# A two-layer attention block on one core: 64 by 64 array tiles in the first attention, and softmax denominators inverted across partitions

## Chip, cores and metric

The kernel runs on one core of one Trainium2 chip. The metric is the device time of one launch in microseconds; the kernel before took 3954.51 us (median of three runs, 3954.51 to 3957.84).

## What is computed

The input is 16 images of 256 channels and 1024 positions in float32. Two layers follow each other for every image:

```python
# layer 0: 4 heads of 64
qkv = (xs @ w_proj + b_proj).reshape(B, S, 4, 3 * 64)
attn = softmax(einsum('bihd,bjhd->bijh', q, k) * 64 ** -0.5, axis=2)
res = einsum('bijh,bjhd->bihd', attn, v).reshape(B, S, 256) @ w_out + b_out + xs
# layer 1: 8 heads of 32
x = x + attention(group_norm(x, gn1_w, gn1_b), qkv_w, proj_w, proj_b, phys_bias)
h = gelu(einsum('oc,bchw->bohw', mlp_w1, group_norm(x, gn2_w, gn2_b)) + mlp_b1)
x = x + einsum('oc,bchw->bohw', mlp_w2, h) + mlp_b2
```

A softmax divides each weighted sum by the sum of its exponentials. That sum, one number for each head and each query position, is called the denominator below.

## The kernel before

Channels lie on the 128 partitions in two chunks (`CC = 2`), positions along the free dimension in blocks of 128 keys (`SB = 8`) and of 512 queries (`NT = 2`). `first_pass` does all the work; `general_pass` runs only if a range test on the denominators fails, which it does not do in the profiled execution. The test needs, for every denominator, a sum of the values and a sum of `exp(-den / 1e-20)`, which the ScalarE instructions at L326 and L329 deliver through `accum_out`; the second of them is called the range exponential below.

**Attention.** One function serves both layers. For a unit (a query block, a channel chunk, a key block) `scores` multiplies keys by queries into a PSUM tile of 128 by 1024 (L267), cut into pieces of 64 output partitions. ScalarE takes the exponential into an SBUF tile `e` (L279). `weigh` multiplies `e` by the values, over all 128 keys at once, into an accumulator bank (L288), and VectorE adds `e` into a running sum `es` (L305). After eight key blocks an item is done: ScalarE copies the accumulator to `res` (L310), and `normalise` follows two ticks later. It multiplies `es` by a matrix of ones, so that every partition of a head gets that head's denominator (L317), copies it out (L326), takes the range exponential (L329), the reciprocal on VectorE over 128 by 512 (L332) and multiplies `res` by it (L333). The second layer uses the same steps with four heads to a chunk and two score tiles per unit.

**Array tiles.** A TensorE instruction names the rows and columns of the array that it uses; the profile shows them as rows*columns. Float32 matmuls show as two instructions each. In the first attention the scores use 64*64 (four side by side), the weighted sums, the denominators and whatever goes through `product` use 128*64 (two side by side). In the second attention it is 32*64 and 128*32. Between the attentions `product` uses 128*128. `product` (L234) cuts its output into pieces of `cols[0]` columns.

**Order.** The image loop runs, for image b: first attention of b; the MLP's first half of image b-1 (`hidden`, L536, 8 pieces); queries, keys and values of layer 1; second attention of b, with pieces filled in between its units (the MLP's second half of b-1, L234 and L561, and the layer-0 projections of b+1). A small class `Later` holds work back by a number of ticks. A tick is one step of the attention generator (three units in the first attention, one in the second) or one piece. So the output projections, `out_proj`, run a few ticks behind their items: `o` for layer 0 and `j` for layer 1. The projection of the first query block of `o` falls near the end of the first attention, that of the second among the `hidden` pieces; the second of `j` falls into the next image's first attention. The tile framework then fixes each engine's instruction order at build time[...].

**Buffers.** PSUM holds three 128 by 1024 tiles, taken in rotation by `wide` (scores, projections, MLP), and two banks, taken by `bank` (accumulators, denominators, group-norm averages). SBUF has eight `e` tiles, four `es` and one `d` tile. SyncE issues the loads of x and the stores of the output and nothing else.

Of the kernel before, what the change touches and what calls it, by code (L numbers as in the profile page):

```python
# [14 lines left out]
P = 128  # L15
# [173 lines left out]
def first_pass(ctx, tc, x, out, k):  # L189
# [7 lines left out]
    work = ctx.enter_context(tc.tile_pool(name="work", bufs=2))  # L197
    small = ctx.enter_context(tc.tile_pool(name="small", bufs=2))
    ps_s = ctx.enter_context(
        tc.tile_pool(name="ps_s", bufs=3, space=bass.MemoryType.PSUM)  # L200
    )
    ps_a = ctx.enter_context(
        tc.tile_pool(name="ps_a", bufs=2, space=bass.MemoryType.PSUM)
    )

    def wide(name):
        return ps_s.tile([P, 2, TB], F32, tag="s", name=name)

    def bank(name):
        return ps_a.tile([P, TB], F32, tag="acc", name=name)  # L210

    blocks = 2 * B * NT * CC
    dsum = act.tile([P, blocks], F32, name="dsum")
    lsum = act.tile([P, blocks], F32, name="lsum")
    block = iter(range(blocks))
# [23 lines left out]

    def attention(layer, b, D, qT, kT, v_of, ones_of, scale, project):
        key = f"{layer}_{b}"
        G = P // D

        items = [(t, c) for t in range(NT) for c in range(CC)]
        if G > 2:
            items.sort(key=lambda tc: tc[1])
        units = [(i, kb) for i in range(len(items)) for kb in range(SB)]
        per = 6 // G
        steps = [units[n : n + per] for n in range(0, len(units), per)]
        res = []
        if G == 2:
            res.append(act.tile([P, CC, S], F32, tag="res", name=f"res_{key}"))
        accs, held, sums = {}, {}, {}  # L260

        def scores(i, kb):
            t, c = items[i]
            tiles = [wide(f"s_{key}_{i}_{kb}_{n}") for n in range(G // 2)]
            for g in range(G):
                for h in range(0, P, HALF):
                    nc.tensor.matmul(  # L267
                        tiles[g // 2][h : h + HALF, g % 2, :],
                        kT[g * D : (g + 1) * D, c, kb * P + h : kb * P + h + HALF],
                        qT[g * D : (g + 1) * D, c, t * TB : (t + 1) * TB],  # L270
                        start=True,
                        stop=True,
                    )
            es = []
            for n, s in enumerate(tiles):
                e = work.tile(
                    [P, 2, TB], F32, tag="e", name=f"e_{key}_{i}_{kb}_{n}", bufs=8
                )
                nc.scalar.activation(e, s, AF.Exp, scale=scale)  # L279
                es.append(e)  # L280
            return i, kb, es

        def weigh(i, kb, es):
            t, c = items[i]
            if kb == 0:
                accs[i] = bank(f"acc_{key}_{i}")
            for g in range(G):
                nc.tensor.matmul(  # L288
                    accs[i][g * D : (g + 1) * D, :],
                    v_of(c * G + g, kb),  # L290
                    es[g // 2][:, g % 2, :],
                    start=(kb == 0),
                    stop=(kb == SB - 1),
                )
            if kb == 0:
                held[i] = es
                return
            if kb == 1:
                sums[i] = [
                    work.tile([P, 2, TB], F32, tag="es", name=f"es_{key}_{i}_{n}", bufs=4)  # L300
                    for n in range(G // 2)
                ]
            for n, e in enumerate(es):
                d = sums[i][n]
                nc.vector.tensor_add(d, held[i][n] if kb == 1 else d, e)  # L305
            if kb == SB - 1:
                if not res:
                    res.append(act.tile([P, CC, S], F32, tag="res", name=f"res_{key}"))
                r = res[0][:, c, t * TB : (t + 1) * TB]
                nc.scalar.copy(r, accs.pop(i))  # L310
                later.after(2, lambda: normalise(i, r))

        def normalise(i, r):
            t, c = items[i]
            den = bank(f"den_{key}_{i}")
            for g in range(G):
                nc.tensor.matmul(  # L317
                    den[g * D : (g + 1) * D, :],
                    ones_of(c * G + g),
                    sums[i][g // 2][:, g % 2, :],  # L320
                    start=True,
                    stop=True,
                )
            at = next(block)
            d = work.tile([P, TB], F32, tag="d", name=f"d_{key}_{i}", bufs=1)
            nc.scalar.activation(  # L326
                d, den, AF.Identity, accum_out=dsum[:, at : at + 1]
            )
            nc.scalar.activation(  # L329
                den, den, AF.Exp, scale=-1.0 / DEN_MIN, accum_out=lsum[:, at : at + 1]  # L330
            )
            nc.vector.reciprocal(d, d)  # L332
            nc.vector.tensor_mul(r, r, d)  # L333
            if c == CC - 1:
                later.after(3, lambda: project(t, res[0]))

        cols[0] = D
        pending = []
        for step in steps:
            now = [scores(*u) for u in step]  # L340
            for p in pending:
                weigh(*p)
            pending = now
            yield
        for p in pending:
            weigh(*p)
        yield
        cols[0] = P

# [21 lines left out]
    def group_norm(key, src, stats, gw, gb, tag, out_tile, wait):  # L371
        st = {}

        def means():
            mv = small.tile([P, CC, 2], F32, tag="mv", name=f"mv_{key}")
            for cc in range(CC):
                nc.vector.bn_aggr(mv[:, cc, :], stats[:, cc].rearrange("p t k -> p (t k)"))
            mean_c = small.tile([P, CC], F32, tag="mean_c", name=f"mean_c_{key}")
            nc.vector.tensor_copy(mean_c, mv[:, :, 0])
            st.update(mv=mv, mean_c=mean_c)  # L380
            later.after(wait, variances)

        def variances():
            ps = bank(f"gm_{key}")
            product(ps[:, :CC], k["gavg"], st["mean_c"], start=True, stop=True)
            mean = small.tile([P, CC], F32, tag="mean", name=f"mean_{key}")
            nc.vector.tensor_copy(mean, ps[:, :CC])

            dv = small.tile([P, CC], F32, tag="dv", name=f"dv_{key}")
            nc.vector.tensor_sub(dv, st["mean_c"], mean)  # L390
            nc.vector.tensor_mul(dv, dv, dv)
            tv = small.tile([P, CC], F32, tag="tv", name=f"tv_{key}")
            nc.vector.tensor_add(tv, dv, st["mv"][:, :, 1])
            st.update(mean=mean, tv=tv)
            later.after(1, apply)

        def apply():
            ps = bank(f"gv_{key}")
            product(ps[:, :CC], k["gavg"], st["tv"], start=True, stop=True)
            rstd = small.tile([P, CC], F32, tag="rstd", name=f"rstd_{key}")  # L400
            nc.vector.tensor_scalar(rstd, ps[:, :CC], EPS, None, ALU.add)
            nc.gpsimd.tensor_tensor(rstd, rstd, k["mhalf"], ALU.pow)
            a = small.tile([P, CC], F32, tag="ga", name=f"ga_{key}")
            nc.vector.tensor_mul(a, rstd, gw)
            ma = small.tile([P, CC], F32, tag="gma", name=f"gma_{key}")
            nc.vector.tensor_mul(ma, st["mean"], a)
            c = small.tile([P, CC], F32, tag="gc", name=f"gc_{key}")
            nc.vector.tensor_sub(c, gb, ma)
            y = act.tile([P, CC, S], F32, tag=tag, name=f"gn_{key}")
            out_tile.append(y)  # L410
            for t in range(NT):
                sl = slice(t * TB, (t + 1) * TB)
                for cc in range(CC):
                    nc.vector.tensor_scalar(  # L414
                        y[:, cc, sl], src[:, cc, sl],
                        a[:, cc : cc + 1], c[:, cc : cc + 1], ALU.mult, ALU.add,
                    )
# [72 lines left out]
    def attention_0(b, qkv_tiles, xb, norm):  # L490
# [3 lines left out]
        def project(t, res):  # L494
# [5 lines left out]
            if t == NT - 1:  # L500
                norm(stats)

        return attention(
            "a", b, D0, q, kk, lambda h, kb: v[:, kb, h], lambda h: k["ones"],
            float(D0) ** -0.5, project,
        )

    def attention_1(b, qkv_tiles, xb, norm):
        q, kk, v = qkv_tiles
# [2 lines left out]
        def project(t, res):  # L512
            out_proj(
                f"j{b}", k["wpj"], CC,
                lambda kc: res[:, kc, t * TB : (t + 1) * TB],
                k["pjb"], xb, t, stats,
            )
            if t == NT - 1:
                norm(stats)

        return attention(
            "b", b, D1, q, kk, lambda h, kb: v[:, kb, h], lambda h: k["eones"][:, h],
            float(D1) ** -0.5, project,
        )

# [70 lines left out]


    def fold_bias():  # L600
        ps = bank("bvo")
        for co in range(CC):
            for kc in range(CC):
                nc.tensor.matmul(
# [11 lines left out]
    for b in range(B):  # L616
# [26 lines left out]
        for m, piece in enumerate(rest):  # L643
# [3 lines left out]
            attention_1(  # L647
                b, tiles1, xs[b],
                lambda st, b=b, hn=hn: group_norm(
                    f"h{b}", xs[b], st, k["g2w"], k["g2b"], "gn", hn, 2  # L650
                ),
            ),
            fill,
# [305 lines left out]
```

## Time and profile before

| | us |
|---|---|
| median of three runs | 3954.51 |
| the profiled execution | 3953.01 |
| its span | 3950.6 |
| PE busy in the span | 3923.9 |
| VectorE busy | 2461.4 |
| ScalarE busy | 2147.3 |
| one image, in the middle of the run (from one image's MLP start on PE, 1030.27, to the next's, 1274.58) | 244.31 |
| first attention of one image, about (PE, 1206.6 to 1274.6) | 68.0 |

The profiled execution spends 2.4 us outside its span. The page gives the engines' busy time, then the span in slices, the DMA queues, the chain of work that ended last, and groups of like instructions by line, engine and tile, with count, summed busy time, and mean duration in ns. The timeline lists an engine's instructions in order of time, with neighbours of one group merged: start, length, engine, line, operation, tiles, shape and count. Matmuls are pipelined, so the length of a merged group runs a little into the next one; differences between the starts of groups are exact.

### The profile page before, as it was taken

What the parts mean: (1) busy time and instruction counts of PE and PEld (TensorE: products, weight loads), DVE (VectorE), ACT (ScalarE), POOL (GpSimd) and SP (SyncE); (2) the same over time, 40 slices, a digit from 0 to 9 for tenths busy, and PEclk for the clock granted to TensorE, in tenths of its full rate; (3) what the DMA queues carried; (4) which work ended last, traced back from release to release, by engine and by line L of the source; (5) the groups of instructions that cost most, each with busy time, mean ns of one, the idle gap of its engine ahead of it and who ended that gap; (6) DMA issues with size and microseconds to landing.
All of it is one profiled execution on the core that took longest, in us unless ns stands there. A gap on an engine that the chain in (4) does not pass through costs nothing.

```text
span 3950.6 us, 77671 instructions
## 1 busy us (share of the span) xinstructions
PE 3923.9 (99%) x34685; PEld 1407.5 (36%) x34685; DVE 2461.4 (62%) x2539; ACT 2147.3 (54%) x2815; POOL 35.3 (1%) x58
## 2 busy tenths in 40 slices
PE   9999999999999999999999999999999999999998
PEld 3324333343333423334233342333424333343335
DVE  4684756847567475674756747567474665747672
ACT  4654645546455464554645546465564655646461
POOL 1000000000000000000000000000000000000000
PEclk9999999999999999999999999999999999999999
DMA  2000000000000000000000000000000000000000
GB/s 75 1 1 7 17 1 23 1 9 15 1 23 1 9 15 1 23 1 12 12 1 23 1 23 1 1 23 1 23 1 4 20 1 23 1 4 10 1 4 20
DMA packets 18501, 42.80 MB, mean 11 GB/s; under 512 B 3728, under 2 KB 5264, under 8 KB 18160
## 3 DMA queue, kind: packets, MB, share of 16 engines
q1 hardware_dynamic: 13824, 33.56, 2.4%
q8 instruction: 273, 4.47, 0.5%
q10 hardware_dynamic: 3712, 3.80, 0.3%
q0 software_dynamic: 624, 0.41, 0.1%
q14 instruction: 68, 0.56, 0.0%
HBM read 20.99 MB, written 16.78 MB: 10 GB/s over the span
## 4 chain that ended last, share of the span: by engine, by line
PE 98%; issue 1%; DVE 1%; DMA 0%; ACT 0%; POOL 0%; POOLq 0%; DVEq 0%
PE s_b L267 14%; PE acc_b L288 12%; PE s_a L267 12%; PE acc_a L288 12%; PE m L536 12%; PE m L234 11%; PE qk_b L234 6%; PE qk_a L234 5%; PE o L234 3%; PE v_a L234 3%; PE v_b L234 3%; PE j L234 3%; PE den_b L317 1%; PE den_a L317 1%; DVE es_b L305 0%
## 5 line engine op out<-in xcount | busy, mean ns | idle before, releaser
L279 ACT ACTIVATE e_b<-s_b 128x1024 f32<-128x1024 f32 x1024 | 994.2, 1025 | 615.7 <-PE s_b L267 608.7
L305 DVE TENSOR_TENSOR es_b<-es_b,e_b 128x1024 f32<-128x1024 f32 x768 | 895.0, 1221 | 296.6 <-ACT e_b L279 296.6
L267 PE MATMUL s_b<-q,k 32*64 32x512 f32 x8192 | 598.3, 613 | 5.0 <-DVE x L364 3.2
L279 ACT ACTIVATE e_a<-s_a 128x1024 f32<-128x1024 f32 x512 | 487.3, 1026 | 180.1 <-PE s_a L267 180.1
L288 PE MATMUL acc_b<-e_b,v 128*32 128x512 f32 x4096 | 546.0, 604 | 0.0
L305 DVE TENSOR_TENSOR es_a<-es_a,e_a 128x1024 f32<-128x1024 f32 x384 | 466.4, 1215 | 32.2 <-ACT e_a L279 5.5
L267 PE MATMUL s_a<-q,k 64*64 64x512 f32 x4096 | 479.8, 598 | 0.0
L288 PE MATMUL acc_a<-e_a,v 128*64 128x512 f32 x2048 | 477.4, 600 | 0.0
L536 PE MATMUL m<-gn_h,w 128*128 128x512 f32 x1024 | 474.8, 605 | 2.0 <-DVE gn_h L414 2.0
L234 PE MATMUL m<-g,w 128*32 128x256 f32 (+1 forms) x7616 | 464.7, 379 | 0.0
L234 PEld LDWEIGHTS m<-g,w 128*32 128x32 f32 (+1 forms) x7616 | 276.1, 112 | 219.1 <-issue 57.8
L544 ACT ACTIVATE g<-m,m1b 128x512 f32<-128x512 f32 x256 | 170.3, 686 | 317.8 <-PE m L536 317.4
L305 DVE TENSOR_TENSOR es_b<-e_b,e_b 128x1024 f32<-128x1024 f32 x128 | 151.1, 1222 | 234.1 <-ACT e_b L279 234.1
L536 PEld LDWEIGHTS m<-gn_h,w 128*128 128x128 f32 x1024 | 186.1, 190 | 256.4 <-issue 190.7
L267 PEld LDWEIGHTS s_b<-q,k 32*64 32x64 f32 x8192 | 144.8, 129 | 361.9 <-issue 178.8
L332 DVE RECIPROCAL d_a<-d_a 128x512 f32<-128x512 f32 x64 | 214.5, 3352 | 64.4 <-ACT d_a L326 64.4
L234 PE MATMUL qk_a<-x,wp 128*32 128x512 f32 (+1 forms) x1856 | 245.2, 594 | 8.8 <-DMA wp<-in_L_conv_w_proj_dram 6.7
L288 PEld LDWEIGHTS acc_a<-e_a,v 128*64 128x64 f32 x2048 | 132.7, 136 | 331.1 <-issue 331.1
L267 PEld LDWEIGHTS s_a<-q,k 64*64 64x64 f32 x4096 | 139.1, 132 | 304.1 <-issue 264.1
L234 PE MATMUL qk_b<-gn_g,wq 128*32 128x512 f32 (+1 forms) x1280 | 236.9, 593 | 0.0
L288 PEld LDWEIGHTS acc_b<-e_b,v 128*32 128x32 f32 x4096 | 82.2, 108 | 406.7 <-issue 402.5
L458 DVE TENSOR_TENSOR v<-v_b,eones 128x512 f32<-128x512 f32 x64 | 44.3, 692 | 276.2 <-PE v_b L234 276.2
(107 smaller groups left out, 2408.8 us busy)
## 6 DMA issues: line engine op xcount, KB each, us to landing
x<-in_x_dram SPq DMA_DIRECT2D x32, 512.0 KB, 4.5
out_dram<-x SPq DMA_DIRECT2D x64, 256.0 KB, 2.0
w<-in_L_conv_mlp_w_dram ACTq DMA_DIRECT2D x2, 1024.0 KB, 14.9
wq<-in_L_conv_qkv_w_dram ACTq DMA_DIRECT2D x1, 768.0 KB, 11.8
wp<-in_L_conv_w_proj_dram ACTq DMA_DIRECT2D x3, 128.0 KB, 9.7
wp<-in_L_conv_w_proj_dram POOLq DMA_DIRECT2D x3, 128.0 KB, 6.9
wo<-in_L_conv_w_out_dram ACTq DMA_DIRECT2D x1, 256.0 KB, 9.3
wpj<-in_L_conv_proj_w_dram ACTq DMA_DIRECT2D x1, 256.0 KB, 13.5
```

Of the source, the lines that this page charges most:

```text
L234: nc.tensor.matmul(o[sl], w[:, sl], r, **flags)
L267: nc.tensor.matmul(tiles[g // 2][h : h + HALF, g % 2, :], kT[g * D : (g + 1) * D, c, kb * P + h : kb * P + h + HALF], qT[g * D : (g + 1) * ...
L279: nc.scalar.activation(e, s, AF.Exp, scale=scale)
L288: nc.tensor.matmul(accs[i][g * D : (g + 1) * D, :], v_of(c * G + g, kb), es[g // 2][:, g % 2, :], start=(kb == 0), stop=(kb == SB - 1),)
L305: nc.vector.tensor_add(d, held[i][n] if kb == 1 else d, e)
L317: nc.tensor.matmul(den[g * D : (g + 1) * D, :], ones_of(c * G + g), sums[i][g // 2][:, g % 2, :], start=True, stop=True,)
L332: nc.vector.reciprocal(d, d)
L458: nc.vector.tensor_mul(d, ps, v_scale.unsqueeze(1).to_broadcast([P, 2, C // D, D]))
L536: nc.tensor.matmul(ps[:, n, :], k["w1"][:, cc, hc * P : (hc + 1) * P], hn[0][:, cc, t * TB : (t + 1) * TB], start=(cc == 0), stop=(cc == C ...
L544: nc.scalar.activation(g, ps[:, n, :], AF.Gelu, bias=k["m1b"][:, hc : hc + 1])
```

## The change

- **The first attention has a function of its own, `attention_a`.** The weighted sums are cut into two halves of 64 keys, each with 64 rows by 64 columns of the array, and the halves go to two PSUM banks. For every even item (counted from 0) the two banks come from `bank`; for every odd item they are the two halves of the third wide tile, which `kept` takes out of the rotation meanwhile. ScalarE copies the first half to `res` and VectorE adds the second. A tick is now one unit; the weighted sums run two units behind the scores.
- **Its denominators** are taken once per query block instead of once per item, with 32 columns and 256 queries to a matmul. `product` uses 32 columns in this stage instead of 64, and the group-norm averages in it use 64 rows by 64 columns.
- **The reciprocal in both attentions** goes through a new helper, `denominators`. ScalarE copies the denominators to `d`. SyncE then issues DMAs that lay one row per head (or half head) over partitions, so that VectorE inverts 128 by 16 instead of 128 by 512; DMAs that gather the results into rows `rr` on partitions 0 to 3; and DMAs that read each such row 64 times (first attention) or 32 times (second) to fill `full`, by which VectorE multiplies `res`.
- **The range exponential** works on `d` in place, after the DMAs that read it.
- **Ticks.** The second query block of `j` is projected in the middle of the next image's first attention, right before a denominator step; the first of `o` in the same attention, some units later; the second of `o` stays among the `hidden` pieces.
- `wide` rotates over three tags by hand; `es` has three buffers instead of four; `res` of layer 1 is two tiles, and the second group norm's output takes the buffer of `q1`.

```diff
+    def denominators(key, d, n, rows, out_to, waits, then, copy):
+        w = d.shape[1] * len(rows) // P
+        spread = work.tile([P, 2 * TB // D0], F32, tag="spread", name=f"sp_{key}", bufs=2)
+        spread = spread[:, :w]
+        rr = work.tile([4, TB], F32, tag="rr", name=f"rr_{key}", bufs=1)
+        full = work.tile([P, n, TB], F32, tag="full", name=f"rd_{key}", bufs=1)
+        at = next(block)
+        copy(at)
+        for p, lo, num, _ in rows:
+            nc.sync.dma_start(
+                spread[lo : lo + num], d[p : p + 1].rearrange("o (a b) -> o a b", b=w)
+            )
+
+        def invert():
+            nc.vector.reciprocal(spread, spread)
+            for *_, parts in rows:
+                for row, c0, lo, num in parts:
+                    nc.sync.dma_start(
+                        rr[row : row + 1, c0 : c0 + num * w].rearrange(
+                            "o (a b) -> o a b", b=w
+                        ),
+                        spread[lo : lo + num],
+                    )
+            for row, lo, num, c in out_to:
+                nc.sync.dma_start(
+                    full[lo : lo + num, c],
+                    rr[row : row + 1].unsqueeze(1).to_broadcast([1, num, TB]),
+                )
+            later.after(waits[1], lambda: then(full))
+
+        def low():
+            nc.scalar.activation(
+                d, d, AF.Exp, scale=-1.0 / DEN_MIN, accum_out=lsum[:, at : at + 1]
+            )
+
+        later.after(waits[0], invert)
+        later.after(waits[2], low)
...
+    def attention_a(b, qT, kT, v, project):
...
+            if kb == 0:
+                if i % 2:
+                    kept.add(2)
+                    acc = wide(f"acc_{key}_{i}", 2)
+                    accs[i] = [acc[:, h, :] for h in range(2)]
+                else:
+                    accs[i] = [bank(f"acc_{key}_{i}_{h}") for h in range(2)]
+            for h in range(2):
+                for g in range(2):
+                    nc.tensor.matmul(
+                        accs[i][h][g * D : (g + 1) * D, :],
+                        v[h * HALF : (h + 1) * HALF, kb, c * 2 + g],
+                        e[h * HALF : (h + 1) * HALF, g, :],
+                        start=(kb == 0),
+                        stop=(kb == SB - 1),
+                    )
...
+                nc.scalar.copy(r, one)
+                nc.vector.tensor_add(r, r, two)
+                kept.discard(2)
+                if c == CC - 1:
+                    later.after(1, lambda: normalise(t))
...
+                        nc.tensor.matmul(
+                            den[j : j + 32, c * half : (c + 1) * half],
+                            k["ones"][:, :32],
+                            sums[t * CC + c][:, g, h * half : (h + 1) * half],
...
+                (2, 3, 5) if t < NT - 1 else (1, 1, 26),
...
+        def scale(t, full):
+            r = res[:, :, t * TB : (t + 1) * TB]
+            nc.vector.tensor_mul(r, r, full)
+            later.after(1 if t < NT - 1 else 3, lambda: project(t, res))
...
+        cols[0] = 32
...
+    def attention_b(b, qT, kT, v, project):
...
-            nc.scalar.activation(
-                d, den, AF.Identity, accum_out=dsum[:, at : at + 1]
-            )
-            nc.scalar.activation(
-                den, den, AF.Exp, scale=-1.0 / DEN_MIN, accum_out=lsum[:, at : at + 1]
-            )
-            nc.vector.reciprocal(d, d)
-            nc.vector.tensor_mul(r, r, d)
...
+            denominators(
+                f"{key}_{i}", d, 1,
+                [(g * D, g * D, D, [(g, 0, g * D, D)]) for g in range(G)],
+                [(g, g * D, D, 0) for g in range(G)],
+                ((3, 3, 7) if b + 1 < B else (1, 1, 5)) if last else (1, 2, 4),
...
+                wait = (12 if b + 1 < B else 1) if last else 1
+                later.after(wait, lambda: project(t, res[t]))
```

## Prediction, made before the changed kernel was run

> **What bounds the kernel now.** I read the page's busy times first, then the chain of work that ended last, then PE's timeline in one first attention, and last the groups that the change touches.
>
> ```profile
> span 3950.6 us, 77671 instructions
> PE 3923.9 (99%) x34685; PEld 1407.5 (36%) x34685; DVE 2461.4 (62%) x2539; ACT 2147.3 (54%) x2815; POOL 35.3 (1%) x58
> PE 98%; issue 1%; DVE 1%; DMA 0%; ACT 0%; POOL 0%; POOLq 0%; DVEq 0%
> ```
>
> PE is never idle and is 98% of the chain. A gain must shorten PE's own stream; any new wait of PE counts in full.
>
> ```profile
> 1005.81 2.81 PE L267 MATMUL s_a<-q,k 64*64 64x512 f32 x24
> 1008.54 2.79 PE L288 MATMUL acc_a<-e_a,v 128*64 128x512 f32 x12
> 1011.27 2.81 PE L267 MATMUL s_a<-q,k 64*64 64x512 f32 x24
> 1014.01 2.80 PE L288 MATMUL acc_a<-e_a,v 128*64 128x512 f32 x12
> 1016.63 1.03 PE L317 MATMUL den_a<-es_a,ones 128*64 128x512 f32 x4
> 1017.59 1.95 PE L267 MATMUL s_a<-q,k 64*64 64x512 f32 x16
> ```
>
> Call one full-array pass of 512 columns a slot: four 64*64 instructions or two 128*64. Scores and weighted sums are six slots each, and each group with one change of tile shape takes 2.73 us (1008.54 - 1005.81). From 1014.01 to 1017.59 there are eight slots, also with one change: 3.58 us. So a slot is (3.58 - 2.73) / 2 = 0.43 us, and a change of shape 2.73 - 6 x 0.43 = 0.16 us.
>
> ```profile
> L332 DVE RECIPROCAL d_a<-d_a 128x512 f32<-128x512 f32 x64 | 214.5, 3352 | 64.4 <-ACT d_a L326 64.4
> L317 PE MATMUL den_a<-es_a,ones 128*64 128x512 f32 x256 | 66.6, 598 | 0.0
> L326 ACT ACTIVATE d_a<-den_a 128x512 f32<-128x512 f32 x64 | 38.3, 598 | 121.7 <-PE den_a L317 121.7
> out_dram<-x SPq DMA_DIRECT2D x64, 256.0 KB, 2.0
> 1206.60:1274.60 68.00, 68.00 (x425) 20.79 (x421) 56.95 (x59) 36.74 (x52) 0.69 (x1) 1.00 0.00 1
> ```
>
> The last line is the first attention of one image: length, then busy us of PE, PEld, VectorE, ScalarE, POOL. VectorE has 57 of 68 us. The line above it is the DMA that I use as the nearest row: 2.0 us from issue to landing for 128 rows of 2 KB. SP spends 0.33 to 0.34 us on issuing one, by the store's own instructions in the trace.
>
> [...]No DMA of this trace reads a single partition[...].
>
> **PE's gain.** I counted the changes of tile shape in the instruction order of both kernels: 1426 before, 1160 after. The 266 that go are those between scores and weighted sums of the first attention. 266 x 0.16 = 43 us. Denominators of the first attention: before 256 instructions, two abreast, 128 slots = 55 us; after, 512 instructions of 256 columns, four abreast, 128 half slots = 27 us. Gain 28 us. Weighted sums: twice the instructions, half the rows, same slots; scores run four abreast at the same slot already, so I add nothing. Together 71 us, 4.4 per image.
>
> **VectorE and ScalarE.** VectorE loses 128 reciprocals of 3.35 us (429 us) and gets 96 of 128x16 (about 0.2 each: 3.35 x 16/512 and a fixed part), 64 additions of a second accumulator half (0.69, as L333) and 32 multiplies of 128x1024 (1.22, as L305) for 64 of 0.69. ScalarE loses 32 copies and 32 range exponentials of the first attention. Neither is the bound; worth nothing while PE's stream covers them. What is new is what they wait for: the range exponential now waits for the DMAs that read `d`, 3 us after the copy, and the next exponentials queue behind it. One or two units of PE work cover that in most places; I put 3 us on the whole run. Odd images have an accumulator tile that was the newest score tile: PE waits for its exponential, about 1.2 us less one score group hoisted ahead (0.86), eight times: 3 us. The SP queue gets 1280 DMAs, 430 us of issue in 3950; the x loads and output stores behind them are needed an image later.
>
> **The path that decides: from denominators to the projection.** After PE's last denominator matmul of the first attention: copy to `d` 0.60 + 0.19 for reading its accumulator + 0.06 = 0.85. Four DMAs to `spread`: 3 x 0.34 + 2.0, landed at 3.9. Reciprocal, 4.1. Eight DMAs to `rr`: issued by 6.8; the first rows have landed by then. Then four DMAs, each reading one row of 2 KB 64 times: 131 KB, all from partitions 0 to 3. Bounds for their time: below, a landing like any other, so the last at about 10.9 (it waits for the last `rr` row, 4.1 + 7 x 0.34 + 2.0 = 8.5, then 0.34 + 2.0)[...]. Neither can be below zero, since the reads are added work. [...]Multiply 1.22: `res` is ready at 28.7 (or 12.1).
>
> PE's order says what it does meanwhile. First query block: six score groups and six weighted groups (24 slots, 10.3), two small averages (0.23 each) and two changes: it reaches `o` at 11.1. Wait 17.6 us (or 1.0). Second block: 18 MLP matmuls of 0.88 (20 instructions in 8.78 us in the chain), 16.0 with the change. Wait 12.7 (or none). Behind each waiting multiply VectorE's additions queue, but PE stands at the same point.
>
> Second attention: the same chain, four broadcasts of 32 x 2 KB[...]. PE reaches `j` of the first block 14.2 us after the denominators (five units, their fillers, seven changes): wait 3.6. Where no projection follows, the late multiply only delays VectorE's additions, and eight `e` tiles hold four units. `j` of the second block comes 19 ticks later, 31 us: hidden.
>
> Sum per image: 17.6 + 12.7 + 3.6 - 4.4 = 29.5, times 16 = 472. The first image's second attention has no fillers, and the last denominators of the run have only a few pieces behind them: about 15 us. 3953.0 + 472 + 15 = 4440; the median of the runs stood 1.5 us above the profiled execution, which I leave out.
>
> **Rivals.** All times against 3953.0.
> (1) [...]the broadcasts land like other DMAs. Then `o` waits 1.0 us per image (16), with 6 for the waits above and about 10 for DMA hops at both ends: 3953 - 71 + 32 = 3914, faster. For it: the 2.0 us of the store, and DMA engines almost idle (2.4% of their time). Against: the store uses all 128 partitions, so it shows nothing of one. It decides where the summed waits come to 4.4 us per image: `res` at 15.5, the last broadcast landing at 14.3[...].
> (2) The full gain, if the hops are shorter than the store's as well: 3953 - 71 + 6 = 3888.
> (3) A port twice as fast[...]: `res` at 19.0, waits 7.9 + 3.0, less 4.4, none at `j`: 16 x 6.5 = 104, and 10: 4067.
> (4) The tile change brings nothing, because the 64*64 sums run slower than a slot (twice the weight loads): against it, the scores do eight loads per 0.86 us at full rate. Small chance, inside the cases above.
>
> **Chances.** Port-bound, about 4440: 0.57. Rival 1: 0.26. Rival 2: 0.07. Rival 3 and others between: 0.10. The measurement can tell about 0.2% (8 us) from none. Rivals 1 and 2 are faster except for a twentieth that other stalls eat; same 0.02; slower 0.67. If the port decides, 4200 to 4580 holds it nine times in ten[...]. The range over both sides goes from 3895 to 4580, which leaves out most of rival 2 and slower ports.
>
> **What would show it.** In the timeline of the changed kernel: score and sum groups in one 64*64 stream, units of 1.72 us apart; `den_a` half as long. In the DMA issues: `rd` with 5 us or more to landing, growing from first to last, up to 20. In the waits: PE's `o` on VectorE's multiply of `res` by `rd`, that multiply on the DMA, 12 to 18 us each, twice per image; a PE share near 87%. It is wrong if `rd` lands within 3 us, or if the multiply is done before PE gets to `o`.

## The result, and the profile after

The changed kernel takes 4906.97 us, median of four runs (4901.65 to 4909.22), against 3954.51 us on the same chip: a ratio of 1.2406, 95% interval 1.2384 to 1.2427. It is slower, by 952 us, and lies outside the predicted range of 3895 to 4580.

The page of the changed kernel: span, busy times, the clock that TensorE was granted in 40 slices, and the chain that ended last by engine and by line.

```profile
span 4904.1 us, 85580 instructions
PE 4086.7 (83%) x37485; PEld 1472.2 (30%) x37485; DVE 2119.1 (43%) x2569; ACT 2140.1 (44%) x2687; POOL 35.3 (1%) x58
PEclk9889989899898998989989899898998989899898
PE 53%; DMA 24%; SPq 11%; DVE 6%; issue 4%; ACT 3%; DVEq 0%; POOL 0%; POOLq 0%; ACTq 0%
```

The clock row of the page before:

```profile
PEclk9999999999999999999999999999999999999999
```

PE falls from 99% of the span to 83%, and from 98% of the chain to 53%: DMAs and their issue on SP have taken a third of it. PE's busy time has risen from 3923.9 us, although it has less to do, and the clock row, all nines before, has eights throughout (mean granted clock 0.916, before 0.998). So there are two losses to explain: idle time, 805 us between PE's first start and its last end (15 before), and slower work.

What PE waited for: total us, times, longest.

```profile
PE o L240 <- DVE res_a L391: 413.1, 25, 21.6
PE gv_h L549 <- DVE tv_h L572: 120.3, 7, 19.6
PE s_b L425 <- DVE x L733: 84.4, 16, 6.4
PE j L240 <- DVE res_b L499: 77.9, 17, 8.1
```

The first row is the forecast wait of the output projection for the multiply. The second is the same wait in disguise: in seven images the multiply stands ahead of the group norm's small operations in VectorE's queue, and PE stops at the norm, one step before `o`. Together 533 us, 33.3 an image.

One first attention, on PE, then SP, then VectorE (start, length; idle time before it in brackets):

```profile
1539.46 1.07 PE L361 MATMUL den_a<-es_a,ones 128*32 128x256 f32 x16 [1.36 <-DVE res_a L348]
...
1551.44 0.28 PE L549 MATMUL gv_h<-tv_h,gavg 64*64 64x2 f32 x4
1572.80 6.47 PE L240 MATMUL o<-res_a,wo 128*32 128x512 f32 x32 [21.07 <-DVE res_a L391]
```

```profile
1541.31 2.40 SPq L260 DMA_DIRECT2D sp_a<-d_a  x4
1545.23 5.17 SPq L268 DMA_DIRECT2D rr_a<-sp_a  x8
1550.50 7.54 SPq L275 DMA_DIRECT2D rd_a<-rr_a  x4
```

```profile
1544.95 0.25 DVE L265 RECIPROCAL sp_a<-sp_a 128x16 f32<-128x16 f32 x1 [1.05 <-DMA sp_a<-d_a]
...
1571.43 1.22 DVE L391 TENSOR_TENSOR res_a<-res_a,rd_a 128x1024 f32<-128x1024 f32 x1 [20.04 <-DMA rd_a<-rr_a]
```

The whole chain can be read off: denominators end at about 1540.3 on PE (the next group starts at 1540.46, after a change of shape), reciprocal at 1544.95, row gathering issued until 1550.4, and 20.9 us from the first broadcast's issue until the multiply may start. PE stands at `o` from 1551.7.

The second attention, PE and then VectorE:

```profile
1722.19 2.01 PE L425 MATMUL s_b<-q,k 32*64 32x512 f32 x16 [5.84 <-DVE x L733]
```

```profile
1719.91 0.69 DVE L499 TENSOR_TENSOR res_b<-res_b,rd_b 128x512 f32<-128x512 f32 x1 [7.73 <-DMA rd_b<-rr_b]
1720.52 1.22 DVE L463 TENSOR_TENSOR es_b<-es_b,e_b 128x1024 f32<-128x1024 f32 x1
1721.65 0.48 DVE L733 SCALAR_TENSOR_TENSOR x<-m,m2b,x 128x256 f32<-128x256 f32 x1
```

VectorE stands for 7.73 us at a multiply whose broadcast has not landed, and what was placed behind it follows only then. Among that is the addition that takes the MLP's result out of a wide PSUM tile (L733), and the next scores need that tile. PE has no projection to do at this point, and waits for the multiply all the same.

Slower work: two stretches of the same image (length; busy us of PE, PEld, VectorE, ScalarE, POOL; then granted clock, DMA share, GB/s).

```profile
1551.50:1572.80 21.30, 0.23 (x5) 0.17 (x5) 1.37 (x2) 0.07 (x1) 0.00 (x0) 0.57 0.77 25
1572.80:1582.70 9.90, 9.90 (x67) 2.84 (x71) 7.53 (x15) 1.66 (x2) 0.69 (x1) 0.71 0.01 2
```

The trace's clock records hold 1.0 and 0.5 alone. The clock is at half for most of the gap (0.57 on average) and still there when work resumes (0.71): `o`, whose 32 instructions take 3.62 us where no gap precedes them (shown below), takes 6.47.

### The profile page after: what moved, and what is told of

It is laid out like the page before. It is cut to its first block, busy times and chain, and to the rows that moved or that the text cites. A ratio compares the mean times of both kernels' runs of the same rounds, so it can differ in the third digit from the quotient of the medians.

```text
span 4904.1 us, 85580 instructions
## 1 busy us (share of the span) xinstructions
PE 4086.7 (83%) x37485; PEld 1472.2 (30%) x37485; DVE 2119.1 (43%) x2569; ACT 2140.1 (44%) x2687; POOL 35.3 (1%) x58
## 3 DMA queue, kind: packets, MB, share of 16 engines
q1 hardware_dynamic: 75264, 68.77, 23.5%
## 4 chain that ended last, share of the span: by engine, by line
PE 53%; DMA 24%; SPq 11%; DVE 6%; issue 4%; ACT 3%; DVEq 0%; POOL 0%; POOLq 0%; ACTq 0%
DMA rd_a<-rr_a 12%; PE s_b L425 8%; DMA rd_b<-rr_b 8%; PE acc_b L446 7%; PE m L240 6%; PE acc_a L331 5%; SPq L268 5%; PE qk_b L240 5%; PE m L708 4%; PE s_a L309 4%; PE o L240 4%; PE qk_a L240 3%; SPq L275 3%; DVE es_a L343 3%; SPq L260 3%
## 5 line engine op out<-in xcount | busy, mean ns | idle before, releaser
L317 ACT ACTIVATE e_a<-s_a 128x1024 f32<-128x1024 f32 x512 | 516.7, 1022 | 700.0 <-PE s_a L309 666.2
L425 PE MATMUL s_b<-q,k 32*64 32x512 f32 x8192 | 641.0, 634 | 99.9 <-DVE x L733 84.4
L331 PE MATMUL acc_a<-e_a,v 64*64 64x512 f32 x4096 | 581.1, 591 | 11.1 <-ACT e_a L317 11.0
L309 PE MATMUL s_a<-q,k 64*64 64x512 f32 x4096 | 587.9, 593 | 0.2 <-DVE res_a L348 0.2
L446 PE MATMUL acc_b<-e_b,v 128*32 128x512 f32 x4096 | 564.0, 623 | 0.0
L240 PE MATMUL o<-res_a,wo 128*32 128x512 f32 (+1 forms) x640 | 185.5, 883 | 413.1 <-DVE res_a L391 413.1
L391 DVE TENSOR_TENSOR res_a<-res_a,rd_a 128x1024 f32<-128x1024 f32 x32 | 39.2, 1225 | 721.7 <-DMA rd_a<-rr_a 721.7
L331 PEld LDWEIGHTS acc_a<-e_a,v 64*64 64x64 f32 x4096 | 176.9, 133 | 304.8 <-issue 226.7
L309 PEld LDWEIGHTS s_a<-q,k 64*64 64x64 f32 x4096 | 171.9, 133 | 286.7 <-issue 220.7
L499 DVE TENSOR_TENSOR res_b<-res_b,rd_b 128x512 f32<-128x512 f32 x64 | 44.3, 693 | 472.3 <-DMA rd_b<-rr_b 472.3
## 6 DMA issues: line engine op xcount, KB each, us to landing
rd_a<-rr_a SPq DMA_DIRECT2D x128, 128.0 KB, 12.8
```

What stands on the lines that cost most here:

```text
L240: nc.tensor.matmul(o[sl], w[:, sl], r, **flags)
L309: nc.tensor.matmul(s[h : h + HALF, g, :], kT[g * D : (g + 1) * D, c, kb * P + h : kb * P + h + HALF], qT[g * D : (g + 1) * D, c, t * TB : ...
L317: nc.scalar.activation(e, s, AF.Exp, scale=float(D) ** -0.5)
L331: nc.tensor.matmul(accs[i][h][g * D : (g + 1) * D, :], v[h * HALF : (h + 1) * HALF, kb, c * 2 + g], e[h * HALF : (h + 1) * HALF, g, :], st ...
L425: nc.tensor.matmul(tiles[g // 2][h : h + HALF, g % 2, :], kT[g * D : (g + 1) * D, c, kb * P + h : kb * P + h + HALF], qT[g * D : (g + 1) * ...
L446: nc.tensor.matmul(accs[i][g * D : (g + 1) * D, :], v[:, kb, c * G + g], es[g // 2][:, g % 2, :], start=(kb == 0), stop=(kb == SB - 1),)
```

## Experiments

My theory after this: the four rows of a block, all on partitions 0 to 3, share one rate of reading (their 524 KB took 20.9 us, 25 GB/s), and that sets the waits; each gap costs, on top, work at half speed after it; and in the second attention the late multiply costs through what is queued behind it. What the rows share is called a port in the prediction, the expectations and the runs' labels; that is an assumption: no run shows what it is. Rivals: issuing or descriptors set the landings, not the rows' place; the slow clock comes from something else than the gaps; the 64 by 64 tiles are slow themselves. Ratios below are to runs of the kernel before on the same chip.

### The rows on partitions 0, 4, 64 and 68

```diff
-        rr = work.tile([4, TB], F32, tag="rr", name=f"rr_{key}", bufs=1)
+        at_row = (0, 4, 64, 68)
+        rr = work.tile([P, TB], F32, tag="rr", name=f"rr_{key}", bufs=1)
...
-                    rr[row : row + 1].unsqueeze(1).to_broadcast([1, num, TB]),
+                    rr[at_row[row] : at_row[row] + 1].unsqueeze(1).to_broadcast([1, num, TB]),
```

> The changed kernel, with the four inverted rows of every block kept on partitions 0, 4, 64 and 68 and no longer on 0, 1, 2 and 3; nothing else differs. Theory ([...]): with four ports the broadcasts of a block land side by side, rd_a's median landing falls from 12.8 us towards 5 to 8, rd_b's from 6.9 towards 4, TensorE's two idle gaps per image ahead of the output projection shrink from about 21 and 13.6 us by 9 us each or more, and the time falls to between 4100 and 4500 us. Rival 1 (the queue's descriptors or SyncE's issuing, 1.9 us a broadcast, set the landings): landings and time stay where they are, within 2% of 4907. Rival 2 (it is the slow clock, not the port): landings fall, but the time by no more than the landings themselves, under 100 us.

Measured: 4374.46 us, ratio 1.1059 (1.104 to 1.1077), 533 us less than the changed kernel. Landings of the changed kernel, then of this one (KB each, median us from issue):

```profile
rd_a<-rr_a SPq DMA_DIRECT2D x128, 128.0 KB, 12.8
rd_b<-rr_b SPq DMA_DIRECT2D x256, 64.0 KB, 6.9
```

```profile
rd_a<-rr_a SPq DMA_DIRECT2D x128, 128.0 KB, 8.2
rd_b<-rr_b SPq DMA_DIRECT2D x256, 64.0 KB, 4.0
```

What is left of the first attention's waits in this run:

```profile
PE o L240 <- DVE res_a L392: 206.2, 25, 13.6
PE gv_h L550 <- DVE tv_h L573: 74.3, 7, 11.1
```

The same bytes land sooner, 8.2 us after issue and not 12.8, with nothing changed but the partitions of the source rows. The second attention's two large waits, for `j` and for the MLP's addition, shrink to 5 us each. The first attention's are 280 us, and two things hold them up. SP still takes 5.2 us to issue the eight gathering DMAs, as before. And from the first broadcast's issue to the multiply it is 12.6 us for four, against 20.9, not a quarter of it: the shortest landing is 6.3 us (131 KB at the 25 GB/s of the changed kernel would be 5.2, an estimate), and the copies don't start together. In the changed kernel SP is held up within the issue of a block's broadcasts:

```profile
L275 SPq DMA_DIRECT2D rd_a<-rr_a x128: 527/964/4730, 74.8 to 4625.2; - x128
```

These are the shortest, median and longest of 128 issues in ns. By their order, the first of a block takes 0.54 us on average, the second 0.61, the third 1.42, the fourth 4.68. With the rows on 0, 4, 64 and 68 the longest of the 128 still takes 3.89, against 4.73. No run shows what SP waits for there.

### The rows on partitions 0, 2, 32 and 34

```diff
-        at_row = (0, 4, 64, 68)
+        at_row = (0, 2, 32, 34)
```

> The changed kernel, with the four inverted rows on partitions 0, 2, 32 and 34[...]. Port theory: nothing changes, rd_a lands at about 12.8 us, 4907 us within 1%. Rival (the broadcasts are slow because the rows are neighbours, whatever the port): as fast as the experiment with partitions 0, 4, 64 and 68.

Measured: 4904.93 us, ratio 1.2403 (1.2378 to 1.2428), as the changed kernel.

```profile
rd_a<-rr_a SPq DMA_DIRECT2D x128, 128.0 KB, 12.6
rd_b<-rr_b SPq DMA_DIRECT2D x256, 64.0 KB, 6.7
```

So it is not their being neighbours that makes the rows slow: on 0, 2, 32 and 34 the median landing is 12.6 us, as on 0 to 3 (12.8), and on 0, 4, 64 and 68 it is 8.2. That the first two sets would behave alike was assumed and not shown before; the two runs agree with it. No other sets were tried, so where the line between slow and fast ones lies isn't shown.

### Second attention back on VectorE

```diff
-            denominators(f"{key}_{i}", d, 1, ...)
+            d = work.tile([P, TB], F32, tag="d", name=f"d_{key}", bufs=1)
...
+            nc.vector.reciprocal(d, d)
+            nc.vector.tensor_mul(r, r, d)
```

> The changed kernel with one part undone: in the second attention the denominators are inverted on VectorE over the full 128x512 tile and multiplied at once, as before the change; the DMA way stays in the first attention alone. Theory (my step that gave the second attention's late multiplies a cost of nothing was wrong): its waits of TensorE go, that is 84 us (s_b behind x), 78 us (j behind res_b) and some 25 us behind e_b and es_b, and with them the slow clock after some 35 gaps, about 2.3 us each or 80 us: 4907 - 265 = 4640 us, from 4590 to 4700. Rival (the second attention is covered, as the prediction had it apart from j's 3.6 us an image): 4907 - 58 = 4850 us or more.

Measured: 4631.17 us, ratio 1.1715 (1.1696 to 1.1735). Undoing the second attention's part alone gives back 276 us, where my prediction had it cost 58. (The edit also projects the first block of `j` two steps later.) PE's waits for `j` are gone, and the one for the MLP's addition is nearly so. By the traces PE's idle time falls by 156 us and its busy time by 118, so the slower work is a large part of what the second attention cost. The first attention's wait, now always seen at `o`, stays, and is 39 us longer.

```profile
PE o L240 <- DVE res_a L401: 572.6, 32, 23.0
...
PE s_b L435 <- DVE x L729: 1.9, 2, 1.0
```

### Useless work in the gaps, twice

Products of operands that lie ready are written into the projection's own PSUM tile ahead of it and are overwritten by it. First 18 and 12 of them for the two blocks, then 26 and 16, with the norm's means one unit earlier.

```diff
     def out_proj(key, w, nk, src, bias, xs, t, stats, fill=0):
         ps = wide(f"{key}_{t}")
+        for _ in range(fill):
+            product(ps[:, 0, :], w[:, 0, 0:P], xs[:, 1 - t, (1 - t) * TB : (2 - t) * TB],
+                    start=True, stop=True)
```

> The changed kernel with work added: ahead of each output projection of the first attention, TensorE multiplies operands that lie ready into the same PSUM tile, 18 full-size products for the first block and 12 for the second, which the projection then overwrites. They fit into the idle gap of 21 and 13.6 us and shorten no wait. Theory (after an idle gap the clock is granted at half, so that the projection and what follows run slow, about 3 us lost for each gap and more in its neighbourhood): the time FALLS by 60 to 150 us, to 4760 to 4850, though 480 products of 0.86 us (413 us of TensorE) are added, and the time at the half clock shrinks from 829 us to about half. Rival (the matmuls after the gap are slow for another reason, or the clock is lost through load and not through idleness): the time stays within 10 us or rises.

Measured: 4989.55 us, ratio 1.2624 (1.2603 to 1.2645). The time rose by 83 us: my forecast was wrong, and the rival's came in. PE's timeline shows why:

```profile
1574.66 15.66 PE L240 MATMUL o<-x,wo 128*32 128x512 f32 x144
1595.72 6.54 PE L240 MATMUL o<-res_a,wo 128*32 128x512 f32 x32 [5.40 <-DVE res_a L391]
```

Here the filling left 5.4 us of gap, and `o` was as slow after that (6.54 us) as after 21 (6.47). The mean granted clock rose from 0.916 to 0.948, since the filling now ran where PE had stood, but PE's busy time, 4487.5 us, still exceeded its work (3923.9 - 71 + 413) by 222, where the changed kernel's exceeded it by 234. And in the seven images where PE stops at the norm's means, the filling came after the gap and was simply added.

> The experiment that fills the gaps ahead of the output projections, with more of the useless products that the projection overwrites: 26 and 16 for the two blocks, so that TensorE has no gap there, and the second group norm's means one unit earlier, so that they no longer queue behind the multiply. 672 products of 0.86 us are 578 us of added work. Theory (a gap of 4 us or more costs, beside itself, 2.2 to 2.9 us of slow clock after it, however long it is; a gap that is closed costs nothing after it): o's 32 matmuls take 3.6 us again and not 6.5, the stretches at half clock fall from 75 to under 45, and the time is 3853 of work at full clock + 578 + some 250 of idle time left + 80 of slow clock, about 4780 us, from 4720 to 4840, less than with 480 products (4990). Rival (the projection is slow for its own sake): o still takes 6 us or more, and the time is over 4860.

Measured: 4880.60 us, ratio 1.2354 (1.2333 to 1.2375).

```profile
1547.85 22.52 PE L240 MATMUL o<-x,wo 128*32 128x512 f32 x208
1570.18 3.62 PE L240 MATMUL o<-res_a,wo 128*32 128x512 f32 x32
```

With the gap closed, `o` takes 3.62 us. All 640 instructions of `o`, in the changed kernel and here (shortest, median and longest in ns):

```profile
L240 PE MATMUL o<-res_a,wo x640: 592/1057/1223, 97.1 to 4652.3; 128*32 128x512 f32 x128, 128*128 128x512 f32 x32
L240 PE MATMUL o<-res_a,wo x640: 592/592/1222, 98.7 to 4620.6; 128*32 128x512 f32 x128, 128*128 128x512 f32 x32
```

Their mean falls from 883 ns to 764 with the weaker filling, and their median is 592 here. The mean granted clock is 0.974, with the weaker filling 0.948. The time is 109 us below the weaker filling, with 165 us more of work in it. But it is 100 us over my figure, and so above the 4860 that I had given to the rival: 8 of 32 projections still waited, idle time was 278 us and not 250, and PE's busy time exceeded its work by 153 us and not by 80. What speaks against the rival is `o` itself, which is at full speed. So the filling shows that the slow work is caused by the gap; it doesn't fix its price to better than that.

### The first projection later

```diff
-                (2, 3, 5) if t < NT - 1 else (1, 1, 26),
+                (2, 13, 5) if t < NT - 1 else (1, 1, 26),
...
+                nc.vector.tensor_scalar(one, newest[0][:, 0, 0:1], 0.0, 1.0, ALU.mult, ALU.add)
+                nc.vector.scalar_tensor_tensor(r, r, one, full, ALU.mult, ALU.mult)
```

> The kernel with four ports, with the first block's multiply and its output projection ten units later in the first attention, so that projection stands where the chain of DMAs has landed. To hold the order, the multiply takes one more factor, a column of ones made from the newest exponential. Theory (the length of the chain against its cover decides, and nothing else is wrong with the placing): TensorE's wait for the first block, 12.3 us an image counting the group norm's means queued behind the multiply, goes, with the 2.4 us that the slow clock takes after it: 4374 - 16 x 14.7 = 4140 us, from 4100 to 4190; the second block's wait of about 5 us stays, since only the MLP's five pieces cover it. Rival (the wait is given back later, in the MLP or at the next projection): over 4250.

Measured: 4158.81 us, ratio 1.052 (1.0502 to 1.0537), 216 us under the rows on 0, 4, 64 and 68 alone. The two blocks of one image:

```profile
1336.28 3.67 PE L240 MATMUL o<-res_a,wo 128*128 128x512 f32 x8 [1.26 <-DVE res_a L399]
...
1364.58 3.78 PE L240 MATMUL o<-res_a,wo 128*128 128x512 f32 x4 [5.24 <-DVE res_a L401]
```

Of the first wait 1.3 us an image are left, and the gain is close to the 235 us that I expected, so little was given back elsewhere; the second wait stays. So where the projection stands matters beside the length of the chain.

### Tiles alone, four versions

The first attention on 64 by 64 tiles with split accumulators, but denominators per item, reciprocals of 128x512 on VectorE and no DMA, as before the change.

> One part of the change alone: the first attention's scores, weighted sums and split accumulators on 64 by 64 tiles as in the changed kernel, but the denominators, their range exponential, the 128x512 reciprocals and the multiplies in both attentions as in the kernel before, with no DMA. 1219 shape changes of TensorE against 1426 before. Theory (the tiling itself is sound and worth 0.16 us for each change of shape saved): 207 x 0.16 = 33 us less than before, 3921 us, from 3910 to 3935, and a clock near 1. Rival 1 (the 64 by 64 stream is slower than the stream it replaces): over 3960. Rival 2 (VectorE, with some 57 us of work in a first attention of about 66 us, becomes the bound there because the split accumulators add to it): 3940 to 4010, with waits of TensorE on VectorE in the first attention.

Measured: 4044.60 us, ratio 1.0228 (1.0211 to 1.0245), slower than my theory and than the second rival (up to 4010), and in the band of the first (over 3960). But score and sum groups still started 0.86 us apart, so it was not the stream that was slow. Four kinds of wait stood out: PE's scores and norm averages on VectorE's queue (14 and 21 us), and the MLP and the projection on ScalarE (13 each), which loaded the tables of Gelu and of the exponential by turns (1.28 us each). An excerpt of the next version's edit:

```diff
-            den = wide(f"den_{key}_{i}")[:, 0, :]
+            den = bank(f"den_{key}_{i}") if i != 1 else wide(f"den_{key}_{i}")[:, 0, :]
...
-                later.after(3, lambda: normalise(i, r))
+                later.after(1 if i == len(items) - 1 else 3, lambda: normalise(i, r))
...
-            later.after(1 if cols[0] == P else 2, apply)
+            later.after(1 if cols[0] == P else 3, apply)
```

> The kernel with the 64 by 64 tiles alone, rid of its own waits: denominators and the group norm's means go to the small PSUM tiles that lie free, the norm's two steps run further apart, the last block's denominators come before the first Gelu, so that the exponential's table is loaded once. 1293 shape changes of TensorE against 1426 before. Theory (the tiling is sound; the 89 us that the first version of it lost were waits of the norm, about 53 us counted from start to start, and of the MLP behind table loads, about 45): 133 x 0.16 = 21 us under before, 3933 us, from 3920 to 3955. Rival (a 64 by 64 stream costs VectorE or PSUM turnover that no placing removes): 3980 or more.

Measured: 4027.30 us, ratio 1.0191 (1.0174 to 1.0208). That is above my range and in the rival's (3980 or more). Those waits went, and another took their place:

```profile
PE s_a L273 <- DVE res_a L312: 47.6, 16, 3.6
```

Once per image the scores wait until VectorE, behind in its queue, has taken the second half out of the wide accumulator. My prediction had no such term: its 3 us were for the other end, where the accumulator waits for the exponential to release that tile. The next version, in part:

```diff
+                if i % 2:
+                    half = work.tile([P, TB], F32, tag="half", name=f"half_{key}_{i}", bufs=1)
+                    nc.scalar.copy(half, two)
+                    two = half
                 nc.vector.tensor_add(r, r, two)
```

> The second version with the 64 by 64 tiles alone, with its two remaining waits taken away: after each odd item ScalarE copies both halves of the wide accumulator out, so that the tile no longer waits for VectorE's addition (3.6 us an image, and some 2.5 us of slow clock behind that gap), and the last block's denominators stand one MLP piece later, with the range exponential read from the copy at the end of the MLP (0.9 us an image). 1242 shape changes of TensorE (the version before it has 1233, and not the 1293 that I wrote) against 1426. Theory (tiling alone is worth 0.16 us for each shape change saved, and the wide accumulator's release was what hid it): 184 x 0.16 = 29 us under before, 3923 us, from 3915 to 3940, faster than both kernels. Rival (VectorE's load in the first attention shows up elsewhere when that wait goes): 3950 or more.

Measured: 3962.18 us, ratio 1.0022 (1.0014 to 1.0031). That is 65 us less than the second version (by the traces 48 of idle time, 19 of busy time): these waits, and the slow clock behind the longer one, were real costs. But 3923 was not reached, and the time lies in the rival's band (3950 or more). The last version, in part:

```diff
                 kept.discard(2)
+                turn[0] %= 2
...
-                later.after(2 if i == len(items) - 1 else 3, lambda: normalise(i, r))
+                later.after(3, lambda: normalise(i, r))
...
-        ps = wide(f"{key}_{t}")
+        if in_banks:
+            ps = [bank(f"{key}_{t}_{co}") for co in range(CC)]
```

> The third version with the 64 by 64 tiles alone. In the second one the slow clock is gone, yet it is 8 us over the kernel before: three gaps an image are left, 0.96 us for the wide accumulator's copy, 1.38 us for the last denominators behind VectorE's sum, 0.84 us for the output projection behind a Gelu that holds its tile, up to 3.2 us or 51 us in all. Here scores use the other two tiles first after an odd item, the last denominators come one MLP piece later, and the last projection writes the two small PSUM tiles. 1279 shape changes against 1426. Theory (shape changes saved are worth 0.16 us each, once nothing waits): 147 x 0.16 = 24 us under before, 3930 us, from 3920 to 3945. Rival (a stream of 64 by 64 tiles at one unit a time gives the saving back in waits wherever they are removed, because units follow each other with less slack than three at a time): 3950 or more.

Measured: 3936.43 us, ratio 0.9959 (0.9946 to 0.9973): 17 us faster than the kernel before, and the fastest kernel here.

```profile
span 3932.8 us, 81970 instructions
PE 3910.7 (99%) x36733; PEld 1452.4 (37%) x36733; DVE 2506.1 (64%) x2633; ACT 2191.1 (56%) x2847; POOL 35.2 (1%) x58
```

PE is as full as before and does less: its busy time is 13 us under that of the kernel before; the rest of the gain is idle time. This is within my range, and ends the rival that the tiles lose wherever they are placed. The tiling pays somewhat less than my sum for its saved changes of shape (24 us; 11 to 21 measured), once nothing waits for it.

## Why the prediction was right and wrong

The forecast was a loss through slow broadcasts (25 GB/s measured), and so it came, but only half of the loss was in the sum: 487 us over the profiled execution, where the spans differ by 953. Two steps failed. The second attention's late multiplies were put at nothing where no projection follows, and work after a wait was taken to run at full speed. Term by term:

- **PE's gain** (71 us): no run shows it whole. The 64 by 64 stream ran at the slot's rate, units 1.72 us apart, as assumed, which ends rival 4. The denominators of a query block take 1.00 us from start to start (1539.46 to 1540.46), against twice 0.96 before: 29 us in the run, 28 forecast. The last version with tiles alone gave 11 to 21 us for 147 changes of shape saved, 24 by my price, which is thus somewhat high.
- **The port**: the time held. 20.7 us from the first broadcast's issue to the last landing was forecast, which no trace had shown; 20.9 were measured, which is 524 KB at 25 GB/s. Rivals 1, 2 and 3 fall with it. The two runs with the rows elsewhere show that their place decides; what limits them there was not shown.
- **The rest of the chain**: I took 0.33 to 0.34 us for SP to issue a DMA, from the stores. The small DMAs took 0.60 to 0.65 (2.40 us for four, 5.17 for eight), and all 1280 took 942 us of SP's time, where I had 430. Their landings were shorter than the 2.0 us that I took from the store, 1.7 in the median. The broadcasts began 10.2 us after the denominators, not 6.8. PE reached `o` after 11.4 us, forecast 11.1. So the first wait was 21 us and not 17.6, the second 13.6 and not 12.7; 533 us for the run against 485.
- **"The late multiply only delays VectorE's additions"**: this step failed. I asked who waits for the additions into `es`, and not what else stands behind the multiply in VectorE's queue. There stood the instruction that frees a PSUM tile (84 us). With `j` (78 us, 58 forecast), smaller waits and the clock after them, the second attention cost 276 us: undoing it gave that back.
- **Small waits**: I had 3 us each for the waits behind the range exponential and for the odd images' tile, and 15 for both ends of the run. The waits that I had not priced, or priced so, came to 183 us by the list of PE's waits: the 84 above, 32 of `m` for a Gelu, 40 of the denominators, 26 of scores and sums for an exponential.
- **The clock**: this step failed too, by being absent. I added waits as if work after them ran at full speed. By the mean clock of 0.916, (1 - 0.916) x 2 x 4904 = 824 us passed at half clock, by the clock records 829. Of these 485 lie in the gaps and cost nothing by themselves; the other 344 held work and cost half of it, 172 us, an estimate for work at half its rate (the median instruction of `o` took 1057 ns, and 592 with the gaps filled). PE's busy time, 4086.7, is 234 over the 3923.9 - 71 that it should be; the remaining 62 may be short stalls that modelled ends hide, which no run isolates.

The differences add up: 48 for the first attention's waits, 20 for `j`, 162 for unpriced waits, 234 for slower work: 464 of the 466 us that the prediction lacked. This is bookkeeping from one trace. What ties the terms to their causes are the experiments, and for the small waits and the 62 us there is none.

In the traces of both kernels the stretches at half clock are multiples of 3.41 us (one to seven of them), the last one of a run excepted. Of the changed kernel's gaps, counted from start to start, all 65 of 4 us or more were followed by half clock within the next 9 us, 4.4 us of it on average (4.1 after those of 4 to 7 us, 4.6 after the 32 over 12). Below that it isn't settled by the gap's length alone. Of six lone gaps of 2.85 to 2.9 us five were followed by half clock. In the second version with tiles alone PE waited 16 times for the wide accumulator, 3.0 us on average: after one such wait (until 1518.8) the clock was 0.67 over the next 5.1 us, but 0.996 over the run, which is some 32 us at half clock in all.

## What to carry over

A wait of TensorE is priced with what follows it: for a gap of 4 us or more, add about 2.2 us of lost work (an estimate, half of the 4.4 us at half clock measured after the 65 of them), almost whatever its length (4.1 us after the shorter, 4.6 after the longest). Shortening a gap from 21 to 5.4 us did not save that (`o` took 6.54 us after it); closing it did (3.62). When an instruction is moved behind a DMA, go through everything queued after it on its engine and ask which of it frees a buffer that TensorE needs. For rows that are broadcast by DMA, try where they lie: on partitions 0, 4, 64 and 68 they landed after 8.2 us in the median, on 0 to 3 after 12.8. Their chain should be counted with SP's issue time for each DMA, 0.60 to 0.65 us for the small ones here, and the consumer be placed where the whole chain has passed.

## What the runs showed of the hardware

- Four broadcasts of 131 KB from rows on partitions 0 to 3 took 20.9 us. In the wait for them (1551.5 to 1572.8) the DMA busy share was 77% while 25 GB/s were moved; in a stretch of the second attention (1722.2 to 1729.1) it was 11%, at 40 GB/s. With the rows on 0, 4, 64 and 68 the 68.77 MB of the same queue took 13.6% of the 16 engines' span (4377.0 us), with 0 to 3 23.5% (of 4904.1). So a high share doesn't show that the DMA engines move much.
- SP's issue of a DMA took 0.33 to 0.34 us for a store of 256 KB and 0.60 to 0.65 us for the small DMAs of the chain. For the fourth broadcast of a block it took 4.68 us on average from rows on 0 to 3; the longest of the 128 took 4.73 there, and 3.89 from rows on 0, 4, 64 and 68. No run separates what these times consist of.
